# Query and value products of an attention layer as seven products of halves

## The chip, the cores and the metric

The kernel runs on one core of one Trainium2 chip. The metric is the device time in microseconds, as the median of several runs. The engines are named as in the profile: PE (TensorE, matrix products), DVE (VectorE), ACT (ScalarE), POOL (GpSimd) and SP (SyncE, which here only issues DMA transfers). Each engine works through its own queue of instructions in order; semaphores tie them together.

## The reference

The layer is a gated cross attention followed by a gated mixture of experts, all in float32. There are 16 sequences of 256 tokens with 512 features, and a context of the same shape.

```python
def xattn(h, ctx, Wq, Wkv):                   # h is the layernorm of x
    query = h @ Wq
    key, value = split(ctx @ Wkv, 2, axis=-1)
    w = softmax(query @ key.T / sqrt(512))
    return w @ value

def ffn(x, gate_w, gate_b, w1, b1, w2, b2, w3, b3):   # x is normalised
    probs = softmax(x @ gate_w + gate_b, over the tokens of a sequence)
    vals, idx = top_k(probs, 2)               # 2 of 8 experts for each token
    y[e] = relu(relu(relu(x @ w1[e] + b1[e]) @ w2[e] + b2[e]) @ w3[e] + b3[e])
    v[e] = sum over all tokens of y[e] * (token's weight for e)
    return for each token the sum of v[e] over its experts

x = x + tanh(g_xattn) * xattn(layernorm(x), ctx, Wq, Wkv)
x = x + tanh(g_ffn) * ffn(layernorm(x), ...)
```

The expert stage's sums run over the whole batch, so it needs lists of the tokens of each expert.

## The kernel before

**Stages.** The 4096 tokens are worked on in 8 groups (`NG`) of 512 (`G`), that is, two sequences (`b` 0 and 1) or four tiles of 128 tokens (`t`). The attention stage is one loop over the groups; the feed-forward stage then takes the tokens sorted by expert in blocks of 528, with weights loaded per block. There each layer (`layer`) already multiplies by Strassen's scheme, with the helpers `add`, `sub`, `part` and `sums`.

**Order.** The order of instructions on PE, ACT, DVE and SP is the order of the program (`tc.manual_schedule` with `ORDER = {PE, ACT, DVE, SP}`). POOL is not in that set: the framework's scheduler orders it. The framework adds semaphores by the regions that instructions read and write.

**The attention loop.** At the start, `merge` multiplies the query and key weights into one matrix `m_sb` (512x512), so that scores are (x m) ctx. One iteration for group g, in PE's order:

- `scores(now, b)` for both sequences: 16 products with 256 columns, from `qT` and the context `ctxT`. DVE takes the maximum (`nmax`, L620) and a bias (L623), ACT the exponentials (L627). `send_exps` and `bring_exps` send these through DRAM and back in quarters, the first half of a transpose.
- `begin(g + 1)`: SP issues the loads of the next x transposed (`xT`), context (`ctxT`) and x, 1 MB each. Both transposed inputs have two buffers (`xTs`, `ctxTs`).
- For the previous group (`last`): `logits` (needs `xnT`), `soften` and `divide` (ACT L245, DVE, ACT L252, DVE).
- `values(now, t)` for four tiles: 4 products of 512 columns into one PSUM bank each, copied out by ACT (L655). Between them stand the routing of the previous group, `show_probs`, `choose`, `count` and `place` (13 small DVE operations, then the slots, then eight indirect list writes by POOL, L323), and `turn_exps`, the second half of the transpose, on DVE.
- `mix(now)`: exponentials by values, 8 products of 512 columns; DVE adds the result to x (L695) and takes the statistics of the new rows (L709, L710). At the end `deviations` forms `veps` on DVE (L183) and `rstd` on POOL (L185).
- `normalise(now)`: DVE scales the rows (L207), SP stores them to `tokens` (L212) and loads them back in quarters (`xq`, L217). `scales(after)` takes the statistics of the next x (L176, L177, L183, and L185 on POOL). `turn_rows(now)` transposes `xq` into `xnT` on DVE (L228).
- `query(after, oc)` for four tiles: 4 products of 512 columns with `m_sb` as the stationary operand, copied out by ACT (L605).

The loop runs over groups 0 to 6. In its last iteration (`g == GA`, 6) a copy of the lists is made and `tabulate_early` runs on DVE before the mix. The last group is written out behind the loop, with the first block of the feed-forward stage between its steps: `gather` fetches rows into the tile `xr` of the pool `rows1`, `send_rows` and `bring_rows` take them through DRAM into `xr_q`, and `turn` transposes them.

**PSUM.** The pool `ps_m` has four banks (`mm`), taken in turn by values, mix and queries.

Of the kernel before, what the change touches and what calls it, by code (L numbers as in the profile page):

```python
# [8 lines left out]
F32 = mybir.dt.float32  # L9
# [7 lines left out]
ALU = mybir.AluOpType  # L17
# [9 lines left out]
def flamingo_gated_layer(  # L27
# [85 lines left out]
    def load_x(g):  # L113
        nc.sync.dma_start(
            xg[g], x_f[g * G : (g + 1) * G, :].rearrange("(t p) d -> p t d", p=P)
        )
# [53 lines left out]
    lists_m = dram.tile([ROWS, 2], I32, name="lists_m")  # L170
    def norms(g, tag):

        mv = stat.tile([P, TG, 2], F32, tag=f"mv{tag}", name="mv")
        for t in range(TG):
            st = stat.tile([P, 6], F32, tag="bn", name="bn")
            nc.vector.bn_stats(st, xg[g][:, t, :])  # L176
            nc.vector.bn_aggr(mv[:, t, :], st)  # L177
        return mv

# [342 lines left out]
    raw = ctx.enter_context(tc.tile_pool(name="raw", bufs=3))  # L522
    weights = {}
    held = {}
    ORDER = {PE, ACT, DVE, SP}
# [3 lines left out]
    with (  # L529
# [22 lines left out]

        def inputs(g):
            xT = xTs[g % 2]
            nc.sync.dma_start(xT, x_ct[:, :, g * G : (g + 1) * G])
            ctxT = ctxTs[g % 2]
            nc.sync.dma_start(ctxT, c_ct[:, :, g * G : (g + 1) * G])
            load_x(g)
            return xT, ctxT

# [26 lines left out]
        def begin(g):  # L587

            s = Group()
            s.g = g  # L590
            s.xT, s.ctxT = inputs(g)
            return s

        def scales(s):

            s.scale = deviations(norms(s.g, "a"), "a", float(D))

# [118 lines left out]
        clear_lists()  # L716
        merge()
        scales(now)
        for oc in range(NC):
            query(now, oc)  # L720
        last, who, rows = None, {}, {}
        for g in range(NG):
            if g + 1 == NG:
                break
            for b in range(BG):
                scores(now, b)
                send_exps(now, b)
                bring_exps(now, b)
            after = begin(g + 1)
            if last:  # L730
                logits(last)
                soften(last)
                divide(last)
            weigh(now)
            values(now, 0)
            values(now, 1)
            if last:
                show_probs(last)
                choose(last)
            turn_exps(now, 0)  # L740
            values(now, 2)
            turn_exps(now, 1)
            if last:
                count(last)
                place(last)
            if g == GA:
                nc.sync.dma_start(
                    lists_a.rearrange("(p r) k -> p r k", p=P),
                    lists.rearrange("(p r) k -> p r k", p=P),
                )  # L750
                tabulate_early()
            values(now, 3)
            mix(now)
            normalise(now)
            scales(after)
            turn_rows(now)
            for oc in range(NC):
                query(after, oc)
            last, now = now, after
# [35 lines left out]
    with (  # L795
# [15 lines left out]
        def load_weights(b):  # L811
# [8 lines left out]
            return wbc[:, :, 1].bitcast(F32)  # L820

        def add(out, a, b):
            nc.vector.tensor_tensor(out, a, b, ALU.add)  # L823

        def sub(out, a, b):
            nc.vector.tensor_tensor(out, a, b, ALU.subtract)  # L826

        def part(w, i, j):
            n, d = NC // 2, D // 2
            return w[:, n * j : n * (j + 1), d * i : d * (i + 1)]

# [329 lines left out]
```

## Time and profile before

| | |
|---|---|
| runs | 1035.89, 1036.77, 1035.90 us; median 1035.9 |
| profiled execution | 1035.96 us, its span 1034.2 us, mean granted clock 0.984 |
| busy time in the span | PE 990.3 us (96%), PE weight load 708.0 (68%), DVE 636.7 (62%), ACT 352.9 (34%), POOL 181.7 (18%) |
| attention, from the first scores to the feed-forward's first product | 36.57 to 378.45 us |
| products of queries (L601) and of values (L651) | 256 instructions each, 111.2 and 114.9 us |
| DMA | 176 MB at 171 GB/s on average |

A line of a timeline gives the start in us, the duration in us, the engine, the line of the kernel, the operation with its output and inputs, the shapes and the number of instructions merged; in brackets the idle time ahead of it and what ended it. Busy times of PE are modelled: matmuls are pipelined. `SPq` is the queue of DMA issues. Each float32 matmul is two instructions on PE.

### The profile page before, as it was taken

What the parts mean: (1) busy time and instruction counts of PE and PEld (TensorE: products, weight loads), DVE (VectorE), ACT (ScalarE), POOL (GpSimd) and SP (SyncE); (2) the same over time, 40 slices, a digit from 0 to 9 for tenths busy, and PEclk for the clock granted to TensorE, in tenths of its full rate; (3) what the DMA queues carried; (4) which work ended last, traced back from release to release, by engine and by line L of the source; (5) the groups of instructions that cost most, each with busy time, mean ns of one, the idle gap of its engine ahead of it and who ended that gap; (6) DMA issues with size and microseconds to landing.
All of it is one profiled execution on the core that took longest, in us unless ns stands there. A gap on an engine that the chain in (4) does not pass through costs nothing. (4 is left out here: it accounts for less than half of the span.)

```text
span 1034.2 us, 11778 instructions
## 1 busy us (share of the span) xinstructions
PE 990.3 (96%) x3872; PEld 708.0 (68%) x3872; DVE 636.7 (62%) x1395; ACT 352.9 (34%) x846; POOL 181.7 (18%) x212
## 2 busy tenths in 40 slices
PE   7999999999999988899999999999999999999964
PEld 3545545455554556688878888888888888888852
DVE  3144554644547486677687766766766766766734
ACT  1212112121221213344444444444444444444421
POOL 2000330303213242022221022112102201200003
PEclk9999999999999999999999999999999999999986
DMA  7165354564544897686776677578578577665108
GB/s 256 38 200 170 82 163 117 173 157 124 162 99 147 216 256 179 188 189 167 191 190 174 185 189 193 181 176 232 158 181 240 151 196 206 163 195 146 63 4 325
DMA packets 156156, 176.41 MB, mean 171 GB/s; under 512 B 38929, under 2 KB 94225, under 8 KB 156050
## 3 DMA queue, kind: packets, MB, share of 16 engines
q1 hardware_dynamic: 145442, 153.42, 53.1%
q0 software_dynamic: 7680, 17.90, 7.1%
q10 hardware_dynamic: 2960, 4.21, 1.1%
q8 instruction: 34, 0.56, 0.2%
q14 instruction: 40, 0.33, 0.1%
HBM read 136.33 MB, written 39.77 MB: 170 GB/s over the span
## 5 line engine op out<-in xcount | busy, mean ns | idle before, releaser
L878 PE MATMUL ps_x<-t,s 128*128 128x264 f32 x768 | 187.0, 387 | 0.0
L878 PEld LDWEIGHTS ps_x<-t,s 128*128 128x128 f32 x768 | 146.4, 191 | 25.1
L466 POOL DMA_INDIRECT xr<-tokens,at_b x80 | 83.6, 1045 | 202.9 <-DMA block<-xr 181.0
L651 PE MATMUL mm<-wv_sb,wide 128*128 128x512 f32 x256 | 114.9, 598 | 0.0
L601 PE MATMUL mm<-early,early 128*128 128x512 f32 x256 | 111.2, 592 | 0.0
L889 ACT ACTIVATE h<-ps_w,bias 128x264 f32<-128x264 f32 x192 | 86.2, 473 | 45.2 <-PE ps_w L878 45.2
L878 PE MATMUL ps_z<-t,w_e 128*128 128x264 f32 x384 | 94.7, 390 | 3.8 <-DVE t L826 3.8
L323 POOL DMA_INDIRECT lists<-pairs,idx x64 | 62.5, 977 | 187.0 <-DVE hot L316 142.4
L878 PE MATMUL ps_x<-t,w_e 128*128 128x264 f32 x384 | 93.3, 386 | 0.0
L601 PEld LDWEIGHTS mm<-early,early 128*128 128x128 f32 x256 | 48.7, 190 | 61.2 <-issue 61.0
L878 PEld LDWEIGHTS ps_z<-t,w_e 128*128 128x128 f32 x384 | 73.8, 192 | 16.9 <-DVE t L826 4.2
L651 PEld LDWEIGHTS mm<-wv_sb,wide 128*128 128x128 f32 x256 | 47.2, 191 | 54.1 <-issue 53.6
L900 ACT COPY u<-ps_x 128x264 f32<-128x264 f32 x96 | 36.3, 378 | 138.5 <-PE ps_x L878 138.5
L823 DVE TENSOR_TENSOR ps_w<-ps_z,u 128x264 f32<-128x264 f32 x96 | 41.4, 438 | 67.9 <-ACT h L889 67.9
L878 PEld LDWEIGHTS ps_x<-t,w_e 128*128 128x128 f32 x384 | 73.1, 190 | 12.5
L826 DVE TENSOR_TENSOR s<-w_e 128x512 f32<-128x512 f32 x96 | 66.1, 689 | 17.0 <-DMA w_e<-in_L_ffn_w 15.4
L823 DVE TENSOR_TENSOR h<-ps_z,u 128x264 f32<-128x264 f32 x96 | 41.4, 431 | 54.7 <-ACT u L909 54.7
L878 PE MATMUL ps_w<-h,s 128*128 128x264 f32 x256 | 64.1, 395 | 5.0 <-DVE ps_w L823 5.0
L889 ACT ACTIVATE h<-h,bias 128x264 f32<-128x264 f32 x96 | 49.5, 515 | 55.6 <-DVE h L823 55.6
L605 ACT COPY wide<-mm 128x512 f32<-128x512 f32 x32 | 18.7, 585 | 139.3 <-PE mm L601 139.3
L878 PE MATMUL ps_x<-h,w_e 128*128 128x264 f32 x256 | 62.3, 387 | 0.0
L878 PE MATMUL ps_w<-h,w_e 128*128 128x264 f32 x256 | 62.2, 386 | 0.0
(151 smaller groups left out, 1323.7 us busy)
## 6 DMA issues: line engine op xcount, KB each, us to landing
w_e<-in_L_ffn_w SPq DMA_DIRECT2D x48, 1024.0 KB, 7.3
xr_q<-block SPq DMA_DIRECT2D x64, 272.0 KB, 8.9
block<-xr SPq DMA_DIRECT2D x16, 1024.0 KB, 8.6
early<-in_x_t SPq DMA_DIRECT2D x8, 1024.0 KB, 5.5
wide<-in_ctx_t SPq DMA_DIRECT2D x8, 1024.0 KB, 7.8
x<-in_x SPq DMA_DIRECT2D x8, 1024.0 KB, 10.0
tokens<-xn SPq DMA_DIRECT2D x32, 256.0 KB, 2.9
xq<-tokens SPq DMA_DIRECT2D x32, 256.0 KB, 5.4
```

Of the source, the lines that this page charges most:

```text
L323: ins = nc.gpsimd.indirect_dma_start(out=lists, out_offset=at, in_=pairs[:, s.g * TG + t, i, :], in_offset=None)
L466: tc.keep_in_program_order(nc.gpsimd.indirect_dma_start(out=r.rows[:n, t, :], out_offset=None, in_=src, in_offset=bass.IndirectOffsetOnAxi ...
L601: nc.tensor.matmul(ps, m_sb[:, c, oc * P : (oc + 1) * P], s.xT[:, c, :], start=(c == 0), stop=(c == NC - 1),)
L605: nc.scalar.copy(qT[:, oc, :], ps)
L651: nc.tensor.matmul(ps, s.ctxT[:, c, t * P : (t + 1) * P], wv_sb[:, c, :], start=(c == 0), stop=(c == NC - 1),)
L823: nc.vector.tensor_tensor(out, a, b, ALU.add)
L826: nc.vector.tensor_tensor(out, a, b, ALU.subtract)
L878: nc.tensor.matmul(ps[o], a[:, k, o * P : (o + 1) * P], b[:, k, :], start=(first and k == 0), stop=(k == 1), skip_group_check=True,)
L889: nc.scalar.activation(out(a, j, o), ps, AF.Relu, bias=x.bias[:, c : c + 1])
L900: nc.scalar.copy(u2[:, o, :], ps_x[o])
```

## The change

Queries of groups 1 to 7 and values of groups 0 to 6 are formed by Strassen's scheme (in Winograd's form, as in the feed-forward stage): both factors are cut into halves of rows and columns, and seven products of 256x256x256 take the place of eight. A new generator `seven` issues them; after each product it yields, so that the caller can put other work between them.

- The factors' sums are formed by DVE, four operations of 128x512 for each factor. Those of the constants `m_sb` and `wv_sb` are formed once (`sum_constants`) and kept in the tiles `xr` and `xr_q`, which are not yet in use. Those of x (`sum_tokens`) stand between `mix` and `normalise`, and overwrite the buffer of the present group's `xT`; those of the context (`sum_context`) stand between the scores of the two sequences, and use the other buffer of `ctxT`.
- So the next context can't be loaded in `begin`: `load_context(after)` is issued when the values are done.
- The first product goes into the bank `ps_x`, is copied to `ps_w` by ACT, and `ps_x` takes the later products on top of it. Partial sums go through ACT copies (`u2`, `u3`) and two DVE additions.
- `show_probs`, `choose`, `turn_exps`, `count` and `place` stand between products of the values. The statistics of the next x (`norms`, now called by `measure`) are split and stand between products of the queries.
- The first group's queries and the last group's values stay as they were.

```diff
@@ -168,14 +168,12 @@
     lists = dram.tile([ROWS, 2], I32, name="lists")
     lists_a = dram.tile([ROWS, 2], I32, name="lists_a")
     lists_m = dram.tile([ROWS, 2], I32, name="lists_m")
-    def norms(g, tag):
-
-        mv = stat.tile([P, TG, 2], F32, tag=f"mv{tag}", name="mv")
-        for t in range(TG):
+    def norms(g, mv, tiles):
+        for t in tiles:
             st = stat.tile([P, 6], F32, tag="bn", name="bn")
             nc.vector.bn_stats(st, xg[g][:, t, :])
             nc.vector.bn_aggr(mv[:, t, :], st)
-        return mv
     def deviations(mv, tag, times=1.0):
@@ -521,6 +519,42 @@
     raw = ctx.enter_context(tc.tile_pool(name="raw", bufs=3))
     weights = {}
+    def add(out, a, b):
+        nc.vector.tensor_tensor(out, a, b, ALU.add)
+    def sub(out, a, b):
+        nc.vector.tensor_tensor(out, a, b, ALU.subtract)
+    def part(w, i, j):
+        n, d = NC // 2, D // 2
+        return w[:, n * j : n * (j + 1), d * i : d * (i + 1)]
+    def sums_of_a(a, s):
+        s1, s2, s3, s4 = s
+        sub(s3, a(0, 0), a(1, 0))
+        add(s1, a(1, 0), a(1, 1))
+        sub(s2, s1, a(0, 0))
+        sub(s4, a(0, 1), s2)
+    def sums_of_b(b, t):
+        t1, t2, t3, t4 = t
+        sub(t1, b(0, 1), b(0, 0))
+        sub(t2, b(1, 1), t1)
+        sub(t3, b(1, 1), b(0, 1))
+        sub(t4, b(1, 0), t2)
+    def quarters_of(w):
+        return [w[:, n, :].rearrange("p (k d) -> p k d", k=2) for n in range(4)]
     held = {}
     ORDER = {PE, ACT, DVE, SP}
     in_order = ExitStack()
@@ -550,13 +584,9 @@
                 nc.sync.dma_start(wq_sb[:, c, :], weight(wq_t)[:, c, :])
                 nc.sync.dma_start(wk_sb[:, c, :], weight(wk_t)[:, c, :])
-        def inputs(g):
-            xT = xTs[g % 2]
-            nc.sync.dma_start(xT, x_ct[:, :, g * G : (g + 1) * G])
-            ctxT = ctxTs[g % 2]
-            nc.sync.dma_start(ctxT, c_ct[:, :, g * G : (g + 1) * G])
-            load_x(g)
-            return xT, ctxT
+        def load_context(s):
+            s.ctxT = ctxTs[s.g % 2]
+            nc.sync.dma_start(s.ctxT, c_ct[:, :, s.g * G : (s.g + 1) * G])
         def merge():
@@ -588,12 +618,109 @@
             s = Group()
             s.g = g
-            s.xT, s.ctxT = inputs(g)
+            s.xT = xTs[g % 2]
+            nc.sync.dma_start(s.xT, x_ct[:, :, g * G : (g + 1) * G])
+            if g == 0:
+                load_context(s)
+            load_x(g)
             return s
+        def measure(s, tiles):
+            if 0 in tiles:
+                s.mva = stat.tile([P, TG, 2], F32, tag="mva", name="mv")
+            norms(s.g, s.mva, tiles)
         def scales(s):
-            s.scale = deviations(norms(s.g, "a"), "a", float(D))
+            s.scale = deviations(s.mva, "a", float(D))
+        sums_m = quarters_of(rows1.tile([P, LT, D], F32, tag="xr", name="sums_m"))
+        sums_v = quarters_of(
+            rows1.tile([P, SBT, P], F32, tag="xr_q", name="sums_v")[:, :16, :].rearrange(
+                "p (n t) d -> p n (t d)", n=4
+            )
+        )
+        def seven(s, a, b, sa, sb, put, add_to):
+            n = D // 2
+            def bank():
+                return ps_m.tile([P, 2, n], F32, tag="mm", name="mm")
+            def product(ps, x, y, first):
+                for o in range(2):
+                    for k in range(2):
+                        nc.tensor.matmul(
+                            ps[:, o, :], x[:, k, o * P : (o + 1) * P], y[:, k, :],
+                            start=(first and o == 0 and k == 0), stop=(k == 1),
+                            skip_group_check=True,
+                        )
+            u2, u3 = (work.tile([P, 2, n], F32, tag=f"u{i}", name="u", bufs=1) for i in range(2))
+            ps_w, ps_z = bank(), bank()
+            ps_x = bank()
+            s1, s2, s3, s4 = sa
+            t1, t2, t3, t4 = sb
+            product(ps_x, a(0, 0), b(0, 0), True)
+            nc.scalar.copy(ps_w, ps_x)
+            yield
+            product(ps_z, s1, t1, True)
+            yield
+            product(ps_x, s2, t2, False)
+            nc.scalar.copy(u2, ps_x)
+            yield
+            product(ps_w, a(0, 1), b(1, 0), False)
+            put(0, 0, ps_w)
+            ps_y = bank()
+            yield
+            add(ps_y, ps_z, u2)
+            product(ps_x, s3, t3, False)
+            nc.scalar.copy(u3, ps_x)
+            yield
+            add_to(ps_z, u3)
+            product(ps_y, s4, b(1, 1), False)
+            put(0, 1, ps_y)
+            yield
+            product(ps_x, a(1, 1), t4, False)
+            put(1, 0, ps_x)
+        def sum_constants():
+            sums_of_a(lambda i, j: part(m_sb, i, j), sums_m)
+            sums_of_b(lambda i, j: part(wv_sb, j, i), sums_v)
+        def sum_tokens(s):
+            s.sx = quarters_of(xTs[1 - s.g % 2])
+            sums_of_b(lambda i, j: part(s.xT, 1 - j, i), s.sx)
+        def sum_context(s):
+            s.sc = quarters_of(ctxTs[1 - s.g % 2])
+            sums_of_a(lambda i, j: part(s.ctxT, i, j), s.sc)
+        def queries(s):
+            def out(i, j):
+                return part(qT, 1 - j, i)
+            return seven(
+                s, lambda i, j: part(m_sb, i, j), lambda i, j: part(s.xT, 1 - j, i),
+                sums_m, s.sx, lambda i, j, ps: nc.scalar.copy(out(i, j), ps),
+                lambda ps, u: add(out(1, 1), ps, u),
+            )
+        def all_values(s):
+            s.v = acts.tile([P, TG, D], F32, tag="v", name="v")
+            def out(i, j):
+                return part(s.v, j, i)
+            return seven(
+                s, lambda i, j: part(s.ctxT, i, j), lambda i, j: part(wv_sb, j, i),
+                s.sc, sums_v, lambda i, j, ps: nc.scalar.copy(out(i, j), ps),
+                lambda ps, u: add(out(1, 1), ps, u),
+            )
         def query(s, oc):
             ps = ps_m.tile([P, G], F32, tag="mm", name="mm")
@@ -715,47 +842,64 @@
         nc.sync.dma_start(wv_sb, weight(wv))
         clear_lists()
         merge()
+        measure(now, range(TG))
         scales(now)
         for oc in range(NC):
             query(now, oc)
+        sum_constants()
         last, who, rows = None, {}, {}
         for g in range(NG):
             if g + 1 == NG:
                 break
-            for b in range(BG):
-                scores(now, b)
-                send_exps(now, b)
-                bring_exps(now, b)
+            scores(now, 0)
+            send_exps(now, 0)
+            bring_exps(now, 0)
+            sum_context(now)
+            scores(now, 1)
+            send_exps(now, 1)
+            bring_exps(now, 1)
             after = begin(g + 1)
             if last:
                 logits(last)
                 soften(last)
                 divide(last)
             weigh(now)
-            values(now, 0)
-            values(now, 1)
+            steps_v = all_values(now)
+            for _ in range(4):
+                next(steps_v)
             if last:
                 show_probs(last)
+            next(steps_v)
+            if last:
                 choose(last)
-            turn_exps(now, 0)
-            values(now, 2)
-            turn_exps(now, 1)
+            for b in range(BG):
+                turn_exps(now, b)
+            next(steps_v)
             if last:
                 count(last)
                 place(last)
+            for _ in steps_v:
+                pass
+            load_context(after)
             if g == GA:
                 nc.sync.dma_start(
                     lists_a.rearrange("(p r) k -> p r k", p=P),
                     lists.rearrange("(p r) k -> p r k", p=P),
                 )
                 tabulate_early()
-            values(now, 3)
             mix(now)
+            sum_tokens(after)
             normalise(now)
+            steps_q = queries(after)
+            for _ in range(5):
+                next(steps_q)
+            measure(after, range(2))
+            next(steps_q)
+            measure(after, range(2, TG))
             scales(after)
+            for _ in steps_q:
+                pass
             turn_rows(now)
-            for oc in range(NC):
-                query(after, oc)
             last, now = now, after
@@ -819,23 +963,6 @@
             issued.append(ins)
             return wbc[:, :, 1].bitcast(F32)
-        def add(out, a, b):
-            nc.vector.tensor_tensor(out, a, b, ALU.add)
-
-        def sub(out, a, b):
-            nc.vector.tensor_tensor(out, a, b, ALU.subtract)
-
-
-
-
-
-
-
-
-        def part(w, i, j):
-            n, d = NC // 2, D // 2
-            return w[:, n * j : n * (j + 1), d * i : d * (i + 1)]
-
         def sums(x):
             w = x.ws[len(x.sums)]
```

## The prediction

> **What bounds the kernel now.** I read the page first, its busy slices:
>
> ```profile
> PE   7999999999999988899999999999999999999964
> PEclk9999999999999999999999999999999999999986
> ```
>
> TensorE (PE) is busy nearly throughout. A PE that shows as busy can still be waiting for operands, so I asked next for one stretch from scores to scores, for group 3:
>
> ```profile
> 166.33:210.59 44.26, 44.26 (x136) 22.68 (x135) 23.11 (x67) 8.23 (x20) 9.78 (x10) 1.00 0.49 141
> ```
>
> The columns are length, busy time of PE, PE weight load, VectorE (DVE), ScalarE (ACT) and GpSimd (POOL), granted clock, DMA share, GB/s. Five iterations in a row last 44.26 us to the hundredth, at clock 1.00. PE's timeline shows why:
>
> ```profile
> 166.33 7.07 PE L614 MATMUL sc<-wide,wide 128*128 128x256 f32 x32
> 173.33 1.92 PE L238 MATMUL pt<-xnT,gw 128*32 128x256 f32 x16
> ...
> 186.56 3.60 PE L651 MATMUL mm<-wv_sb,wide 128*128 128x512 f32 x8
> 189.99 7.03 PE L690 MATMUL mm<-v,eT 128*128 128x512 f32 x16
> 196.86 13.90 PE L601 MATMUL mm<-early,early 128*128 128x512 f32 x32
> ```
>
> No line has a wait. Each f32 matmul is two instructions. The queries take 210.59 - 196.86 = 13.73 us for 32 instructions, 0.429 each. Scores with 256 columns: 36.57 to 43.48 in the first group, 6.91/32 = 0.216 each. Every PE microsecond removed here is worth one, as long as nothing else becomes late. So I read what is nearly late, on VectorE, POOL and ACT:
>
> ```profile
> 198.79 0.17 DVE L183 TENSOR_SCALAR veps<-mv 128x4 f32<-128x4 f32 x1
> 200.19 1.92 DVE L207 TENSOR_SCALAR xn<-x,mv,rstd 128x512 f32<-128x512 f32 x4 [1.23 <-POOL rstd L185]
> ...
> 212.73 2.31 DVE L228 STREAM_TRANSPOSE xnT<-xq 128x2048 f32<-128x2048 f32 x1 [7.22 <-DMA xq<-tokens]
> ...
> 197.96 0.96 POOL L323 DMA_INDIRECT lists<-pairs,idx  x1 [0.30 <-issue]
> 199.11 1.04 POOL L185 TENSOR_TENSOR rstd<-veps,neg_half 128x4 f32<-128x4 f32 x1 [0.19 <-DVE veps L183]
> ...
> 175.51 0.46 ACT L245 ACTIVATE pr<-pt,gb 64x256 f32<-64x256 f32 x1
> 176.45 0.51 ACT L252 ACTIVATE pr<-pr,gmax 64x256 f32<-64x256 f32 x1 [0.48 <-DVE gmax L250]
> ```
>
> A chain runs from normalise (200.19) through the tokens' round trip in DRAM to the transpose in turn_rows (212.73): 12.5 us (12.2 to 12.7 in five of seven groups). It now ends 4.4 us after the scores begin, and logits need it 7.0 after. POOL reaches rstd when its eight list writes, 1.26 apart, are done.
>
> **What the change saves.** A product of halves is 8 instructions of 256 columns: 8 x 0.216 = 1.73 us, seven are 12.09. Saved per product 13.73 - 12.09 = 1.64 us. Queries of groups 1 to 7 and values of groups 0 to 6 change: 14 x 1.64 = 23.0 us if nothing waits. The weight load (190 ns of 216) stays hidden, as in the feed-forward stage, which already runs such products at 1.78 us for 264 columns.
>
> **What it costs, in PE's order.** T is the start of mix (L690), S of scores.
>
> Queries. The second product needs t1, the first of sum_tokens, which VectorE does after mix's statistics and L183: done at T + 8.97 (198.96 - 189.99). With 0.69 us for a 128x512 subtraction (L826) t1 is there at T + 9.75. PE has done mix (6.87) and the first product at T + 8.6: a **stall of 1.2 us**. Bounds: 0.9 (subtraction at 0.49, the 128x512 L569) to 1.3. The later sums come every 0.65 to 0.73 against 1.73 of PE. The sum into ps_y stands behind normalise on VectorE, which ends below T + 15; PE needs it at T + 16.7: hidden.
>
> Place. Values now take 12.09 instead of 13.73, and add_to(ps_z, u3), 0.75 us by the nearest PSUM row (L695), stands ahead of place on VectorE; the last product, not two tiles, follows count. The first list write moves from T - 0.9 to T + 1.75, the last ends at T + 11.8. If POOL's order stays (list writes first, as in every group), rstd is ready at T + 12.85; without POOL, sum_tokens would let normalise start at T + 11.65. Now it starts at T + 10.2.
>
> Scores. Normalise at T + 12.85 plus 12.5 gives turn_rows at T + 25.35, ended at T + 27.6. Scores begin at T + 6.87 + 12.09 + 1.2 = T + 20.15. So turn_rows ends at S + 7.5, not S + 4.4. Logits, wanted at S + 6.95, **stall 0.55**. Behind turn_rows VectorE has maximum and bias of batch 0 (0.9), then the four sums of sum_context (2.65), then batch 1 (0.9): S + 11.95. ACT then does exps (1.15), L245, L252 with VectorE's gmax between (1.6): S + 14.7. Only then, in ACT's queue, comes copy(ps_w, ps_x) of the first value product, 0.59 (L655): S + 15.3. The third product accumulates in ps_x again and must wait for that copy. PE is ready for it at 7.5 + 1.85 + 3.45 = S + 12.8: a **stall of 2.5 us**. Before, values had a bank each, and a late copy kept nobody. Bounds: none (sums at no cost and the chain 2 us shorter) to 3.2.
>
> Later products of values wait for copies of 0.6 us with 1.73 us of PE between: hidden. The mix needs the last product's copy 3.4 us later: hidden. load_context moves behind the values on SP's queue: issued at T + 0.3, landing 7.8 us on (median of that load), needed at S = T + 20: hidden by 12 us; what stands behind it on SP, the stores of normalise, isn't due until T + 13. x_t and x stay where they were. The constants' sums (8 x 0.69) run on VectorE while PE does the first queries to 36.57: free. The split measure only moves statistics that fit under the queries.
>
> **Sum by group.** Group 0 has neither logits nor list writes: 3.28 - 1.2 = 2.1 gained. In group 1 turn_rows ends at S + 6.3, since group 0 had no list writes: stalls 1.9 and 1.2, gain 0.2. Groups 2 to 5: 0.55 + 2.5 + 1.2 - 3.28 = 0.95 lost each, 3.8. Group 6 values: 0.55 + 2.5 - 1.64 = 1.4 lost. So its mix starts 2.9 late.
>
> The end of group 6. The feed-forward's first matmul (378.45) hangs on turn_rows of group 6 (349.71): maximum, exps, their round trip, tabulate_more, mix. There tabulate_early (4.9 us on VectorE) follows place, so with place 2.8 later and sum_tokens (2.65) before normalise, less the 1.1 of rstd that runs beneath, normalise starts at T + 16.1, not T + 11.9. Its chain took 15.0 there; at 14.5 turn_rows is 3.7 later against T. All of this reaches the end: 2.9 + 3.7 = **6.6 us lost**. (The feed-forward stage itself is unchanged and PE-bound at 12.5 us a layer, so it passes a shift on.)
>
> **The clock.** Two pairs of neighbouring stretches around PE waits of 1.64 and 2.68 us, cut where the granted clock changes:
>
> ```profile
> 349.06:352.46 3.40, 1.76 (x11) 1.14 (x11) 2.75 (x2) 0.00 (x0) 1.54 (x3) 1.00 0.70 202
> 352.46:355.87 3.41, 3.41 (x21) 1.57 (x16) 1.30 (x5) 2.65 (x9) 2.67 (x3) 1.00 0.94 289
> 376.35:379.76 3.41, 1.31 (x5) 1.18 (x6) 3.38 (x7) 0.00 (x0) 2.75 (x3) 0.95 1.04 381
> 379.76:383.18 3.42, 3.42 (x10) 2.62 (x10) 3.35 (x5) 0.44 (x2) 1.41 (x3) 0.55 1.20 336
> ```
>
> After a stretch with 1.76 us busy of 3.40 the clock stays 1.00; after one with 1.31 of 3.41 it is about half for the next 3.41 us, which costs 1.7 us. A stall of 2.5 us puts 2.1 us into one stretch with a chance of (0.9 + 0.8)/3.41 = 0.5. Of five such stalls I take two: 2 x 1.7 = 3.4 us; bounds 0 and 8.5.
>
> The Trainium skill (TensorE: Matmul & The Clock Gate, "HAM oscillation — how this bites in real kernels") says to avoid idle gaps above some 3.4 us. By that rule stalls of 2.5 us cost no clock and the sum would be 1042.6. The trace shows half clock after 2.68 us, so the row decides.
>
> The profiled execution took 1035.96 us (span 1034.2), beside a median of 1035.9: no correction. 1035.96 + 6.6 + 3.4 = **1046.0 us**. Faster or slower than 0.2% (2.1 us) is about what can be told from no change.
>
> **Rivals.**
> *The late chain isn't as late.* If POOL does rstd ahead of the list writes, or place is earlier, normalise starts at T + 11.65 and turn_rows ends at S + 6.3: no logits stall, third product 1.9. A group loses 1.2 + 1.9 - 3.28, that is, gains 0.2. Sum: -2.1 - 0.2 - 0.8 + 0.25 + 3.7 = +0.9: 1036.8, to 1040 with two slow stretches. For it: nothing fixes POOL's order by hand. Against: every group of before does the list writes first. Chance 0.18.
>
> *Faster: the copy isn't kept waiting.* If turn_rows ends by S + 4.5, batch 1's exps end at scores' end + 2.6 and copy(ps_w, ps_x) is done before the third product is due. That point decides. Then groups 0 to 5 gain 2.1 each and group 6 1.6; with 3.7 lost at the end: -10.5, 1025.5. If the queries' stall vanishes and the end is absorbed too: 1013. For it: VectorE is busy 52% of an iteration only, and the round trip is mostly DMA latency. Against: it was 12.2 us or more in each group. Chance 0.18.
>
> *Worse.* All five stalls and group 1's bring half clock (10.2): 1052.8. Chance 0.09.
>
> **How the numbers follow.** Likeliest case 0.55: 1042.6 to 1051. The range 1031 to 1052 leaves out about 0.2: the lower part of the faster rival and the worse one. Faster by over 0.2%: 0.18 and a little of the first rival, 0.20. Within 0.2%: most of that rival, 0.13. Slower: 0.67.
>
> **What would show it.** Right: products of the new helper 1.73 us apart; waits of PE for VectorE at the queries' second product near 1.2 us; waits for ACT at the values' third product near 2.5 us from group 2 on, and the transpose of turn_rows ending 7 us after scores begin; half-clock stretches before 350 us; the first feed-forward matmul near 388. Wrong: iterations below 43 us without waits of PE for ACT, turn_rows ending before S + 5, or rstd ahead of list writes on POOL.

## Result and profile after

The changed kernel took 1042.9 us as the median of 20 runs (1038.5 to 1049.0), beside 1036.7 for the kernel before (20 runs, 1035.0 to 1041.0). The ratio is 1.0062, with a 95% interval of 1.0047 to 1.0076: slower, by 6.2 us. The profiled execution took 1044.64 us with a span of 1042.9 and a mean clock of 0.981. It is 1.7 us above its median, so the account below, made between two profiled executions, comes to +8.7 us.

The page of the changed kernel: PE's busy slices, and two of the groups (busy time, mean ns, idle time before them and what ended it).

```profile
PE   7999989999898898999999999999999999999964
...
L655 PE MATMUL mm<-sums_v,wide 128*128 128x256 f32 x224 | 56.2, 396 | 11.0 <-ACT mm L667 11.0
...
L655 PE MATMUL mm<-early,sums_m 128*128 128x256 f32 x224 | 52.8, 390 | 9.7 <-DVE early L526 9.7
```

PE's busy time fell from 990.3 to 975.7 us, by 14.6. The products themselves save 14 x 1.64 = 23.0; the half clock (4.8) and what waits cost beside their idle time (some 4), both worked out below, count as busy. Its idle time rose from 43.9 to 67.2 (span less busy time), by 23.3. The difference is the 8.7. The two groups name the new waits: values for the copy L667 on ACT, queries for the sum L526 on DVE. In the slices (26.1 us each) an 8 now stands at 130, 261 and 313 us, where before every slice but the first was a 9 up to 362.

The same stretch as before, scores to scores in group 3:

```profile
164.02:209.02 45.00, 41.56 (x184) 31.61 (x183) 30.72 (x79) 10.46 (x24) 10.28 (x10) 1.00 0.48 141
```

45.00 us instead of 44.26, and PE is idle for 3.44 of it, where it had been idle for none. PE's timeline in that stretch says where (scores start at S = 164.02, mix at T = 188.94):

```profile
171.74 1.92 PE L236 MATMUL pt<-xnT,gw 128*32 128x256 f32 x16 [0.65 <-DVE xnT L226]
...
175.42 1.89 PE L655 MATMUL mm<-sums_v,wide 128*128 128x256 f32 x8
179.23 1.99 PE L655 MATMUL mm<-sums_v,wide 128*128 128x256 f32 x8 [1.92 <-ACT mm L667]
...
195.81 1.89 PE L655 MATMUL mm<-early,early 128*128 128x256 f32 x8
198.56 3.72 PE L655 MATMUL mm<-early,sums_m 128*128 128x256 f32 x16 [0.86 <-DVE early L526]
```

Three waits: 0.65 for the transposed rows ahead of logits, 1.92 ahead of the values' third product, 0.86 ahead of the queries' second. The ACT timeline shows what stood ahead of the copy that the 1.92 is for:

```profile
176.06 0.57 ACT L754 ACTIVATE ex<-sc,nbias,rstd 128x256 f32<-128x256 f32 x1 [2.25 <-PE mm L655]
...
177.16 0.46 ACT L243 ACTIVATE pr<-pt,gb 64x256 f32<-64x256 f32 x1
178.10 0.51 ACT L250 ACTIVATE pr<-pr,gmax 64x256 f32<-64x256 f32 x1 [0.48 <-DVE gmax L248]
...
178.61 0.57 ACT L667 COPY mm<-mm 128x512 f32<-128x512 f32 x1
```

The product that L667 copies was done near 175.5 (173.59 + 1.99), but the copy's turn came at 178.61, behind the softmax (L243, L250) and, ahead of that, batch 1's exponentials (L754), which began at 176.06. Their row names PE as what they waited for, but DVE's bias, which they read, ended only at 175.98, just before them; the first experiment below, which moves nothing but sums on DVE, confirms that it was DVE. DVE's timeline shows why those were late, and the chain behind the mix:

```profile
169.37 2.31 DVE L226 STREAM_TRANSPOSE xnT<-xq 128x2048 f32<-128x2048 f32 x1 [5.48 <-DMA xq<-tokens]
...
173.76 1.42 DVE L526 TENSOR_TENSOR wide<-wide,wide 128x512 f32<-128x512 f32 x2
175.10 0.68 DVE L747 TENSOR_REDUCE nmax<-sc 128x2 f32<-128x512 f32 x1
...
197.82 0.69 DVE L526 TENSOR_TENSOR early<-early 128x512 f32<-128x512 f32 x1
...
201.77 1.91 DVE L205 TENSOR_SCALAR xn<-x,mv,rstd 128x512 f32<-128x512 f32 x4 [1.33 <-POOL rstd L183]
```

Batch 1's maximum (175.10) stands behind the transpose and the four context sums (172.44 to 175.18, the last two of them shown); `normalise` (201.77) waits for POOL. The last two instructions of POOL in that stretch are the eighth list write and `rstd`:

```profile
199.64 1.03 POOL L321 DMA_INDIRECT lists<-pairs,idx  x1 [0.30 <-issue]
200.69 1.04 POOL L183 TENSOR_TENSOR rstd<-veps,neg_half 128x4 f32<-128x4 f32 x1
```

**Half clock.** Two neighbouring stretches around the copy's wait in group 5 (columns as in the prediction's tables: length, PE, PE weight load, DVE, ACT, POOL, clock, DMA share, GB/s):

```profile
266.97:270.38 3.41, 1.48 (x6) 0.91 (x5) 1.51 (x7) 1.86 (x6) 0.00 (x0) 0.92 0.56 154
270.38:273.79 3.41, 3.41 (x11) 2.77 (x10) 0.39 (x1) 0.59 (x1) 0.00 (x0) 0.58 0.47 92
```

After a stretch with 1.48 us busy of 3.41 the clock fell to 0.58 for 3.41 us. Group 6 has the same from 318.17 to 321.58. A third such stretch (clock 0.57) follows a wait of 4.49 us in group 6:

```profile
341.99:345.40 3.41, 3.41 (x9) 2.82 (x10) 3.41 (x7) 0.00 (x0) 0.80 (x1) 0.57 0.32 88
```

```profile
341.94 5.17 PE L655 MATMUL mm<-early,sums_m 128*128 128x256 f32 x16 [4.49 <-DVE early L526]
...
360.85 1.92 PE L236 MATMUL pt<-xnT,gw 128*32 128x256 f32 x16
...
386.54 1.16 PE L1110 MATMUL ps_w<-xnT,ident 128*128 128x264 f32 x4 [2.00 <-DVE x L822]
```

The second view is the end of group 6 on PE's timeline. The queries' second product waits 4.49 us, since `sum_tokens` stands behind `tabulate_early` on DVE. Logits (360.85) no longer wait, as they did for 1.64 us before. The feed-forward's first product comes at 386.54, 8.1 us later than before; the stage behind it adds 0.6.

### The profile page after: what moved, and what is told of

It reads as the page before. It is cut to its first block, busy times and chain, and to the rows that moved or that the text cites. A ratio compares the mean times of both kernels' runs of the same rounds, so it can differ in the third digit from the quotient of the medians.

```text
span 1042.9 us, 12628 instructions
## 1 busy us (share of the span) xinstructions
PE 975.7 (94%) x4208; PEld 771.6 (74%) x4208; DVE 695.5 (67%) x1487; ACT 369.3 (35%) x874; POOL 186.6 (18%) x212
## 5 line engine op out<-in xcount | busy, mean ns | idle before, releaser
L321 POOL DMA_INDIRECT lists<-pairs,idx x64 | 65.2, 1019 | 183.6 <-DVE hot L314 133.8
L523 DVE TENSOR_TENSOR ps_w<-ps_z,u 128x264 f32<-128x264 f32 x96 | 41.4, 439 | 69.7 <-ACT h L1016 69.6
L1005 PEld LDWEIGHTS ps_x<-t,w_e 128*128 128x128 f32 x384 | 73.6, 192 | 12.8
L523 DVE TENSOR_TENSOR h<-ps_z,u 128x264 f32<-128x264 f32 x96 | 41.5, 432 | 54.7 <-ACT u L1036 54.7
L526 DVE TENSOR_TENSOR s<-w_e 128x512 f32<-128x512 f32 x96 | 66.2, 689 | 14.8 <-DMA w_e<-in_L_ffn_w 13.2
L655 PE MATMUL mm<-sums_v,wide 128*128 128x256 f32 x224 | 56.2, 396 | 11.0 <-ACT mm L667 11.0
L655 PE MATMUL mm<-early,sums_m 128*128 128x256 f32 x224 | 52.8, 390 | 9.7 <-DVE early L526 9.7
L1005 PEld LDWEIGHTS ps_w<-h,s 128*128 128x128 f32 x256 | 48.7, 192 | 16.6 <-DVE ps_w L523 8.4
L526 DVE TENSOR_TENSOR t<-h 128x528 f32<-128x528 f32 x64 | 45.1, 705 | 21.4 <-ACT h L1016 20.4
L655 PEld LDWEIGHTS mm<-early,sums_m 128*128 128x128 f32 x224 | 43.0, 195 | 18.3 <-DVE early L526 12.5
```

The lines of the kernel that those rows point to most:

```text
L321: ins = nc.gpsimd.indirect_dma_start(out=lists, out_offset=at, in_=pairs[:, s.g * TG + t, i, :], in_offset=None)
L655: nc.tensor.matmul(ps[:, o, :], x[:, k, o * P : (o + 1) * P], y[:, k, :], start=(first and o == 0 and k == 0), stop=(k == 1), skip_group_c ...
L1005: nc.tensor.matmul(ps[o], a[:, k, o * P : (o + 1) * P], b[:, k, :], start=(first and k == 0), stop=(k == 1), skip_group_check=True,)
```

## Experiments

My theory: the loss is waits. The copy L667 waits in ACT's queue for batch 1's exponentials, held up by the context's sums on DVE; the first sum of the tokens comes too late for the second product; the late chain (list writes, `rstd`, round trip, transpose) makes logits wait. The products themselves are worth 3.28 us an iteration. One rival: the seven products with their copies and additions are no cheaper than the eight, and the waits only stand where something else would wait. Another: POOL's order is what matters, and the rest follows from late rows. Each kernel below starts from the changed one. Medians of the kernel before beside them were 1035.6 (first four), 1036.2 (next four) and 1035.9 (last four).

### The context's sums an iteration earlier

```diff
+        sum_context(now)                # behind sum_constants, for group 0
-            sum_context(now)            # between the scores of the sequences
+            if g + 2 < NG:
+                sum_context(after)      # behind the queries, ahead of turn_rows
```

> Edit: the four sums of the next context move from between the two scores to the end of the iteration, ahead of turn_rows, where VectorE waits 5 us for the tokens' round trip; nothing else changes. Queue theory (the loss is waits of PE that come from the place of single steps in in-order queues): the batch 1 exps and the softmax end 2.65 us earlier, copy(ps_w, ps_x) is done before the third value product is due, the 11.0 us of PE waits for ACT fall below 1 us and the half-clock stretches behind them go (3.4 us); waits for the transpose (4.1 us) and for the first token sum (0.86 us each) stay. 1042.9 - 11 - 3.4: about 1029 us, 1026 to 1032. Rival (VectorE simply has 6 us more work a group, PSUM copies and more weight loads, wherever they stand): the waits reappear elsewhere, 1041 to 1044.

Measured: 1027.9 us, ratio 0.9923 [0.9895, 0.9950]. The waits of PE (total, times, longest) from 20 to 440 us:

```profile
PE mm L655 <- DVE early L526: 9.6, 7, 4.5
...
PE pt L236 <- DVE xnT L226: 3.7, 5, 1.3
```

The line for ACT, 11.0 us in six waits, is gone; the two others stand as they were. By the ratios the kernel is 14.4 us faster than the changed one (0.0139 x 1036), more than the 11.0: the half clock behind two of those waits went too, and a wait costs more than its listed idle time (0.26 us, as the next but one experiment shows). By the traces that is 11.0 + 2 x 1.69 + 6 x 0.26 = 15.9, less 1.6 for a second half-clock stretch at the end of group 6, where the changed kernel's trace has one: 14.3. One move of four DVE instructions in each group decides between slower and faster than before.

### The tokens' sums ahead of the values

```diff
+            after = begin(g + 1)        # x transposed, between the scores
-            after = begin(g + 1)
+            load_x(g + 1)
+            sum_tokens(after)           # ahead of all_values
-            sum_tokens(after)           # behind mix
```

> Edit: the next x transposed is loaded behind the first send_exps instead of behind the second bring_exps, and its four sums are formed behind weigh, ahead of the value products, instead of between mix and normalise. Queue theory: the waits of 0.86 us for the first token sum go in groups 0 to 5 (5.2 us), but POOL still ends its list writes 11.7 us after the mix begins, so rstd and the transpose stay where they are against the mix, and logits in groups 2 to 6 wait 0.9 us longer, about 1.7; waits for ACT stay near 1.9. Net gain 0.86 + 1.5 in groups 0 and 1, and 2.6 us at the end of group 6, where normalise waits for no POOL: 1036 to 1040 us. If instead normalise is held by the sums and not by POOL, logits waits vanish too and it is 1033 or less. Rival (amount of work): 1042 to 1045, the earlier load colliding with the exponentials' round trip.

Measured: 1037.7 us, ratio 1.0012 [0.9994, 1.0031], as expected. The waits for the first sum are gone, those for ACT stay (10.5), and those of logits grow from 4.1 to 9.8.

### Queries alone and values alone

```diff
# queries_alone: values as before (four tiles, own bank each), context loaded in begin, no sum_context
-            steps_v = all_values(now)
+            values(now, 0)
# values_alone: queries as before, no sum_tokens
-            steps_q = queries(after)
+            for oc in range(NC):
+                query(after, oc)
```

> Edit: only the queries are seven products; values, their order and the context's load are as in the kernel before. Queue theory: 7 x 1.64 = 11.5 us saved, waits of 0.86 us at each second product (6 us) stay, no wait for ACT (the four value tiles have a bank each), transpose at most 6.7 us after scores begin so logits hardly wait; 1.6 to 2.6 us lost at the end of group 6 from the sums ahead of normalise. 1036.7 - 11.5 + 6 + 2: about 1033 us. Rival (amount of work): slower than before, about half of the change's loss, 1039 to 1040.

> Edit: only the values are seven products; the queries are four tiles as before, behind the statistics and turn_rows. Queue theory: 11.5 us saved, but place and so rstd on POOL are late (list writes end 11.7 us after the mix begins), the transpose ends 7 us after scores begin, the context's sums follow, and the third product waits about 1.9 us for ACT in groups 1 to 6 (11 us), with about two half-clock stretches (3.4 us); 2 to 3 us lost at the end of group 6. 1036.7 - 11.5 + 11 + 3.4 + 2.5: about 1042 us, 1038 to 1044. Rival (amount of work): about half of the change's loss, 1039 to 1040, spread over all products.

Measured: queries alone 1031.5 us, ratio 0.9966 [0.9948, 0.9985]; values alone 1040.0, ratio 1.0036 [1.0018, 1.0054]. The values alone fall into the range of both theories, so their time decides nothing; their trace has 7.7 us in five waits of the third product for L667, which speaks for the queue. The queries alone decide: the rival had 1039 to 1040. They gain although they wait:

```profile
PE mm L654 <- DVE early L526: 7.8, 7, 2.6
```

```profile
165.01 7.07 PE L740 MATMUL sc<-wide,wide 128*128 128x256 f32 x32
...
208.75 7.07 PE L740 MATMUL sc<-wide,wide 128*128 128x256 f32 x32
```

From scores to scores the iterations of groups 3 and 4 last 43.74 us: 44.26 - 1.64 + 0.86 is 43.48, so the wait of 0.86 costs 0.26 more than the idle time that is listed for it. The effects don't add: -4.2 and +4.3 against before would make none, and the whole change loses 6.2. The queries' sums make `normalise` later, by which the values' waits for ACT grow from 7.7 to 11.0 us.

### Both sums early

```diff
# the edits of the first two experiments together
```

> Edit: both moves together, the context's sums ahead of turn_rows and the tokens' sums behind weigh with the earlier load. Queue theory: no wait for ACT and none for token sums, but POOL still holds rstd until its list writes end, so the transpose keeps its place against the mix while scores begin 0.9 us sooner: logits wait about 1.7 us in groups 2 to 6 (8 us in all). Against the context move alone about 1.7 us gained in groups 0 and 1 and 2.6 at the end of group 6: about 1023 us, 1020 to 1026. If POOL does not hold the chain, logits waits go too: 1017. Rival (amount of work): no better than the context move alone, 1027 to 1030.

Measured: 1036.8 us, ratio 1.0001 [0.9984, 1.0017]: a miss by 14 us. Issue of the next transposed x, and the sum that needs it, on the timelines of SP and DVE:

```profile
131.36 0.47 SPq L622 DMA_DIRECT2D early<-in_x_t  x1
```

```profile
137.29 0.69 DVE L526 TENSOR_TENSOR early<-early 128x512 f32<-128x512 f32 x1 [2.62 <-DMA early<-in_x_t]
```

The load stands on SP behind `send_exps`, which waits for batch 0's exponentials. It is issued 11.1 us after scores begin (120.31) and needs 5.9, and DVE waits for it, 22.3 us in seven waits. What stands behind it on DVE is then late:

```profile
PE pt L236 <- DVE xnT L226: 10.5, 6, 3.7
PE mm L655 <- DVE mm L523: 7.2, 8, 1.4
```

The transpose's wait is that of logits; some 8 of its 10.5 us were in the forecast. L523 is the addition into `ps_y`; its 7.2 us are new, and so are 5.3 us of waits for `picked`, since the routing is late as well. With the 2.5 more for logits that is 15.0, about the miss. I had moved the sums without asking when their load could land. In the second experiment DVE waited for the same load, but only 7.1 us: there the context's sums, 2.7 us, still stood ahead of them on DVE, so that less of the load's time was left to wait for.

### rstd ahead of the last list writes

```diff
-            for t in range(TG): ...     # list writes inside place
+            if last and g < GA:
+                write_lists(last)       # behind mix, POOL held to the program's order
```

> Edit: of the change as it is, only POOL's order: in groups 1 to 5 the reciprocal deviations of the mix are computed ahead of the eight list writes, which are issued behind them. Queue theory: normalise starts as soon as the token sums end (11.0 us after the mix begins instead of 12.8), so the transpose and with it logits, exps and the copy come 1.2 to 1.8 us earlier in groups 2 to 6: waits for the transpose 4.1 us to below 1, for ACT 11 to about 8, perhaps fewer half-clock stretches: 1035 to 1038 us. If POOL's order does not matter (the round trip or VectorE decides): 1042 to 1044.

Measured: 1046.8 us, ratio 1.0100 [1.0078, 1.0122]: a miss, slower than the changed kernel. `normalise` did move, from T + 12.83 to T + 11.83. Of the eight list writes of group 3 seven still went ahead of `rstd` (201.37); the last stands behind it on POOL:

```profile
202.95 1.41 POOL L329 DMA_INDIRECT lists<-pairs,idx  x1 [0.20 <-issue]
```

The rows' stores and loads on SP's queue, in this kernel and then in the changed one:

```profile
203.35 1.81 SPq L212 DMA_DIRECT2D tokens<-xn  x4
209.36 1.91 SPq L217 DMA_DIRECT2D xq<-tokens  x4
```

```profile
202.34 1.81 SPq L210 DMA_DIRECT2D tokens<-xn  x4
206.54 1.91 SPq L215 DMA_DIRECT2D xq<-tokens  x4
```

From stores to loads it is 6.0 us instead of 4.2, and in groups 1 to 5 the way from `normalise` to the transpose takes 13.4 to 14.3 us instead of 12.2 to 13.1. The transpose starts no earlier against the scores (S + 5.1 to 6.1, beside S + 5.0 to 5.9 in the changed kernel). More than the 1.0 us could hardly be had: the tokens' sums, ahead of `normalise` on DVE, end at T + 11.5. So that rival falls: what POOL gave was lost on the round trip. The longer trip comes with this edit elsewhere too: in groups 1 to 5 it is 12.2 to 12.6 us in `both_sums_early` and 14.0 to 14.6 in the next kernel, which adds only this. That the list write beside the stores delays them is likely, and only argued: no run moved it away from them. Why the kernel is 3.9 us slower than the changed one (0.0038 x 1036) is explained in part only: logits wait 0.8 us more, and the trace has four half-clock stretches ahead of 350 us instead of three; the rest stays open.

### All three, and with the table later

```diff
# all_three: both_sums_early and rstd_first together
# all_three_table_later: besides, tabulate_early behind normalise instead of ahead of mix
```

> Edit: both sums moved and rstd ahead of the list writes. Queue theory: in groups 0 to 5 PE waits for nothing (transpose at most 6 us after scores begin, copy done before the third product): 14 x 1.64 = 23 us saved, less what group 6 loses (list writes and table ahead of the mix's statistics there, about 2 us, and its logits): 1014 to 1018 us. Rival (amount of work): waits reappear, 1023 or more.

> Edit: as the three together, and in group 6 the copy of the lists and tabulate_early stand behind normalise instead of ahead of the mix. Queue theory: the mix's statistics and normalise of group 6 start some 5 us earlier on VectorE, POOL then holds rstd to about 11.7 us after the mix begins; the transpose that the feed-forward stage hangs on comes 2 to 3 us earlier, unless the block's rows, whose list is copied later, become the last: 1011 to 1016 us, or the same as the three together if the rows decide.

Measured: 1039.1 us, ratio 1.0018 [1.0005, 1.0031], and 1040.9, ratio 1.0042 [1.0025, 1.0059]. Both miss by over 20 us, for the two reasons just seen: DVE waits 19.0 and 18.5 us for x, logits 13.7 and 10.0, and the trip takes some 14 us in both (13.7 to 14.6 in groups 1 to 5). With the table later, `normalise` of group 6 starts at T + 12.7 instead of T + 14.5, yet the feed-forward's first product is only 1.2 us earlier than without (381.64 against 382.89).

### The copy ahead of the softmax

```diff
             after = begin(g + 1)
+            steps_v = all_values(now)
+            next(steps_v)               # first product and its copy, ahead of logits
             if last:
                 logits(last) ...
-            steps_v = all_values(now)
-            for _ in range(4):
+            for _ in range(3):
                 next(steps_v)
```

> Edit: of the change as it is, only the first product of the values, with its copy on ACT, is issued ahead of logits and the softmax of the previous group. Queue theory (the third product waits because its copy stands behind two softmax steps on ACT and behind late exps): the copy starts when the exps of batch 1 end, 13.2 us after scores begin, instead of 14.6; the product covers the wait of logits. PE's waits in groups 2 to 6 fall from about 0.8 + 1.9 to about 1.6 us each: 4 to 6 us gained, and at 1.6 us no half-clock stretch: 1035 to 1039 us. If the copy's own place in the queue does not matter: 1042 to 1044.

Measured: 1031.1 us, ratio 0.9950 [0.9931, 0.9969], faster than expected. The copy of group 2 on ACT (batch 1's exponentials end at 131.93, the softmax begins at 132.33) and the product that waits for it on PE:

```profile
131.82 0.59 ACT L667 COPY mm<-mm 128x512 f32<-128x512 f32 x1
```

```profile
132.46 1.99 PE L655 MATMUL mm<-sums_v,wide 128*128 128x256 f32 x8 [1.69 <-ACT mm L667]
```

The copy now goes ahead of the softmax; the wait falls from 1.92 to 1.69 only, since batch 1's exponentials still stand before both. But the product ahead of logits covers the late transpose, so the waits of logits are gone, and no wait in groups 1 to 5 is over 1.69: none is followed by half clock.

### Context's sums early, copy first, first sum early

```diff
# context_and_copy_first: context_sums_early and copy_first together
# context_and_first_sum: context_sums_early, and the tokens' first sum by itself:
+            first_token_sum(after)      # t1 alone, ahead of mix
             mix(now)
             sum_tokens(after)           # t2, t3, t4
# context_copy_first_sum: all of these
```

> Edit: the context's sums ahead of turn_rows, and the first value product ahead of logits. Queue theory: the first product (1.73 us) covers the wait of logits (3.7 us in five groups with the context move alone), and the copy is still done in time: 1027.9 - 3.7, about 1024 us, 1022 to 1026. If the transpose's lateness goes on to a later step (softmax, show_probs): 1027 to 1029.

> Edit: the context's sums ahead of turn_rows, and of the tokens' sums only the first (t1) ahead of the mix, where the transposed x has landed; the other three stay behind it. Queue theory: the wait of 0.86 us of the second query product goes (at most 0.3 is left for t2), normalise keeps its time, since POOL holds rstd to 11.7 us after the mix begins; scores come 0.7 us sooner, so logits wait that much longer in groups 2 to 6. Gain in groups 0 and 1 alone, 1 to 2 us: 1026 to 1028 us. If logits do not wait longer: 1022.

> Edit: the context's sums ahead of turn_rows, the first value product ahead of logits, and t1 ahead of the mix. Queue theory: the first product covers the logits' wait also where it is longer (1.5 to 2 us against 1.73 us), so the 0.86 us of the queries' second product are gained in all groups: 1018 to 1022 us, the fastest of all. If the waits only move on: 1024 to 1028.

Measured: 1024.5 us, ratio 0.9891 [0.9870, 0.9913]; 1026.2, ratio 0.9901 [0.9883, 0.9918]; 1022.0, ratio 0.9863 [0.9844, 0.9883]. All as expected. PE's waits in the first of them, and in the last:

```profile
PE mm L655 <- DVE early L526: 10.0, 7, 4.5
```

```profile
PE mm L655 <- DVE x L829: 3.0, 1, 3.0
PE mm L655 <- DVE early L526: 2.0, 2, 1.4
```

In the first, hardly more than the waits for the tokens' first sum is left, and the iterations of groups 1 to 4 last 42.10 us (42.09 in two of them), that of group 2 for one:

```profile
118.32 7.07 PE L741 MATMUL sc<-wide,wide 128*128 128x256 f32 x32
...
160.42 7.07 PE L741 MATMUL sc<-wide,wide 128*128 128x256 f32 x32
```

44.26 - 3.28 + 0.86 + 0.26 is just that. In the second kernel those waits are gone, but logits wait 8.3 us in six waits: the time saved is waited for at the next late step. With all three edits little waiting is left in groups 0 to 5: the iterations of groups 1 to 5 last 41.4 to 42.3 us, and 44.26 - 3.28, without any wait, would be 40.98. This is the fastest version, 13.9 us below the kernel before by the medians. The rival that the products are no cheaper falls: they are worth what was worked out, once nothing waits.

## Why the prediction was right

It said 1046.0 us, slower with 0.67, and the median is 1042.9, at the lower end of its likeliest case (1042.6 to 1051). Between the two profiled executions, up to the mix of group 6 the change lost 5.19 us (forecast 2.9, and 3.4 for the clock), from there to the feed-forward stage 2.90 (3.7), and 0.6 behind it (nothing): 8.7 where 10.0 was forecast. The steps one by one:

**Saving.** 3.28 us an iteration: confirmed to the hundredth by the 42.10 us above; 43.74 - 42.10, with the same wait of 0.86 in both, is the 1.64 of the values by itself.

**Queries' first sum.** 1.2 us forecast, 0.86 listed, 1.12 with what a wait costs beside. The sum came at T + 9.57 (forecast 9.75, though 8.97 + 0.69 is 9.66), and PE was ready at T + 8.76 (forecast 8.6).

**The late chain.** First list write T + 1.4 (forecast 1.75), `rstd` ready T + 12.8 (12.85), `normalise` T + 12.83, trip 12.2 to 13.1 (12.5), transpose ended at S + 7.66 in group 3 (7.5). Logits waited 0.90, 0.65, 0.24, 1.18 and 1.16 us in groups 2 to 6 (0.55). One row was read too simply: in the kernel before, `rstd` waited for `veps` on DVE, which ended at 198.96, as close behind the last list write (198.92) as could be. In the changed kernel `veps` ended at 197.91 and the last list write at 200.67, so there it is the list writes that hold it.

**The copy.** Its end was forecast at S + 15.3 and came at S + 15.16. PE was ready at S + 13.3, not S + 12.8: logits began at S + 7.7 instead of 7.5, and the two products ahead of the wait took 3.72 us instead of 3.45. So 1.92 us instead of 2.5 in groups 2 to 6, and 1.36 instead of 1.9 in group 1. The mechanism was right, and the term too large by 0.5. `context_sums_early` shows both the culprit and its price.

**By group.** Change of each iteration against before; "built up" takes the listed waits, 0.26 more for each wait of a product and 0.06 for one of logits:

| group | forecast | measured | built up |
|---|---|---|---|
| 0 | -2.1 | -2.16 | -2.16 |
| 1 | -0.2 | -0.54 | -0.54 |
| 2 | 0.95 | 1.00 | 0.98 |
| 3 | 0.95 | 0.74 | 0.73 |
| 4 | 0.95 | 0.34 | 0.33 |
| 5 | 0.95 | 2.96 | 1.27, and 1.69 left |
| 6, scores to mix | 1.4 | 3.46 | 1.77, and 1.69 left |
| 6, mix to scores | in the 3.7 | 5.29 | 3.83, and 1.46 left |
| scores to feed-forward | in the 3.7 | -2.39 | -2.38 |

With the 0.61 us by which the scores of group 0 begin earlier (35.96 instead of 36.57), this sums to the 8.1 us at the feed-forward's first product (forecast near 388, measured 386.54).

**The clock.** Two of the five waits were taken to bring half clock at 1.7 us each: two did, in groups 5 and 6, and each left 1.69. The number was a draw that came out; waits of 1.92 or 1.93 us in groups 2 to 4 brought none, and of five waits of 1.92 in `token_sums_early` only one was followed by it. There was luck in it: the prediction asked for 2.1 us of idle time in one stretch, which a wait of 1.92 can't give. The stretches with 1.48 of 3.41 and 1.60 of 3.47 us busy show that 1.9 is enough, so the wait was taken as too long and the threshold as too high, and the two errors cancelled. A third stretch, in the wait of 4.49 us below, was not forecast. The Trainium skill (TensorE: Matmul & The Clock Gate, "HAM oscillation — how this bites in real kernels") speaks of gaps over some 3.4 us; here a wait of 1.93 was followed by half clock, so the measurement decides. That the sum by that rule, 1042.6, is nearer to the median is no support for it.

**The end of group 6: the step that failed.** The prediction had `normalise` later behind `tabulate_early` and `sum_tokens`, and so `turn_rows` 3.7 us late ahead of the feed-forward stage. `normalise` did come at T + 15.8 (forecast 16.1). But PE itself was later still: the second product of the queries needs t1, and t1 stands behind the same `tabulate_early`. It waited 4.49 us, with half clock after it, so that scores of group 7 began 5.29 us later against T. Then the transpose wasn't late any more, logits lost their wait of 1.64 and the feed-forward 0.68 of its wait (2.68 to 2.00): 2.39 given back with the 0.06. The net is +2.9 instead of +3.7, near the forecast by another way: the prediction followed the chain of DVE and forgot to ask the same lateness of the PE product that reads t1. The last version, in which t1 is ahead of the mix, still waits 3.02 us there for the mix's additions (L829) and 1.42 for a later sum.

**load_context** was to be issued at T + 0.3. It was issued at T - 2.0 in group 3 (186.90), as the last product doesn't read the sums' tile; it is hidden either way: no wait for it shows.

**Rivals.** "Rstd ahead of list writes" would have given 1036.8 to 1040 by the prediction; the run gave 1046.8: `normalise` came at T + 11.8, but the trip grew, and the transpose came no earlier. "The copy isn't kept waiting" gave a forecast of 1025.5: the kernel with the context's sums early, in which no product waits for that copy, took 1027.9.

## What to carry to other kernels

When a product saves its time by partial sums, ask for each sum and copy where it stands in its engine's queue and which instruction of the bottleneck reads it; four sums of 0.7 us in each group, put at the wrong place, cost 14 us here, and a place an iteration earlier made the same arithmetic a gain. A bank that later products accumulate in turns its copy from a drain into a link of the chain, so issue that copy ahead of whatever else its engine has to do. And an operation can be moved ahead only as far as its input's load allows: moving the tokens' sums with their load gave back all that the first move had won over the kernel before.

## What the runs showed of the hardware

A wait of PE between products costs more than its listed idle time: 0.26 us more for the 256-column products (43.74 and 42.10 us iterations, to the hundredth), 0.06 for the narrow logits (an iteration of 42.35 us in `context_and_first_sum` with a wait of 1.31: 44.26 - 3.28 + 1.31 is 42.29). It can be seen in the rows of the queries of group 3: from 195.81 to the beginning of the wait (198.56 - 0.86 = 197.70) it is 1.89 us, and the two products behind the wait take 3.56, to 202.12, where undisturbed ones follow each other at 1.73. That is 0.16 and 0.10.

Half clock followed waits of 1.93 us, and 3.41 us of it cost 1.69; of five waits of 1.92 or 1.93 two were followed by it, and none of the five waits for the copy, 0.91 to 1.69, in `copy_first`. In the twenty runs of the changed kernel the two with a mean clock of 0.986 took 1038.5 and 1039.5 us, the others, at 0.979 to 0.983, took 1040.8 to 1049.0. The profiled 1044.64 less what its three half-clock stretches in the attention stage cost (2 x 1.69 + 1.46, 4.8 us) is 1039.8, near those two; that they had none is not shown, as they left no trace.

The round trip of rows through DRAM isn't a constant: in groups 1 to 5 it took 12.2 to 13.1 us in the changed kernel, where the list writes end ahead of it, and 13.4 to 14.3 in `rstd_first`, where the last one is issued beside it. List writes aren't the only cause: in the kernel before, where they end ahead of it, it took 14.2 us in group 4 and 15.0 in group 6.
